# Last stage: the GEGLU's transposes behind the scores, the GEGLU one slot later, and the order of the drain

## The chip, the core and the metric

The kernel runs on one core of one Trainium2 chip, as one launch. The metric is the device time of that launch in microseconds (us). Five engines run beside each other, each in the order of its own instructions: TensorE (PE, whose weight loads the profile lists as PEld), VectorE (DVE), ScalarE (ACT), GpSimd (POOL) and SyncE (SP), which here issues the DMAs. An instruction that needs another engine's result waits on a semaphore, and everything behind it on its own engine waits too.

## The reference

The input x is 8 x 512 x 128, fp32. Two blocks follow each other, each with attention, a residual and a layer norm, then a feed-forward part, a residual and a layer norm. The feed-forward part of the second block, in which the change lies, is itself a small transformer of two layers with windowed attention:

```python
def _layer(x, wqkv, qs, ksc, wo, lg, lb, w1, b1, w2, b2):
    h = shift_token(x)              # half of the features from the token before
    q, k, v = split(h @ wqkv)       # 8 heads of 64
    q, k = l2norm(q) * qs, l2norm(k) * ksc
    q, k = rotary_xpos(q, k)
    x = x + local_attention(q, k, v) @ wo      # windows of 64 tokens and the window before
    h = shift_token(x)
    h = (h - mean) / sqrt(var + 1e-05) * lg + lb
    a, g = split(h @ w1 + b1)       # 341 wide each
    x = x + (a * gelu(g)) @ w2 + b2
    return x
...
x = _layernorm(x + _L1_ffn_ref(x, ...))
```

Its first steps, a layer norm's mean and variance, the product with w1, the gated GELU (GEGLU) and the product with w2, are what the change moves about, together with the last layer norm of all.

## The kernel before, in words

The kernel runs in stages: attention of the first block, its quantized feed-forward part (ffn0), attention of the second block, and the last stage, ffn1, whose function main() holds the change. All activations stay in SBUF: xs and xn, each 128 partitions x 32 chunks of 128 tokens x 128 features. DMAs on the way only move data between partitions.

**Items, chunks and slots.** The last stage has K = 16 items: k = 0 to 7 are the eight batch entries in layer 0, k = 8 to 15 the same in layer 1. An item has NT = 4 chunks of 128 tokens. The loop at L1007 runs over slots t = 1 to 63 with k, c = divmod(t, 4): in one slot each engine gets its instructions for several chunks at different depths of a pipeline. Chunk t begins (the projections to q and k), chunk t-1 is transposed (operands_T), chunk t-2 has its scores and exponentials, chunk t-3 is divided by its sums, chunk t-4 has its weights transposed and multiplied with v, and chunk t-5 gets its output product (sums). All instructions are kept in program order, so the order of the calls in the loop's body is the order on each engine.

**What a slot has, in order.** begin (L1004: PE, q_ps and k_ps), weights_T (L888: PE, p_ps), rotate of q (L713: DVE), over_sums (L865: DVE reciprocal den, POOL product pw), weights_taken (L894: DVE copies pT), scores (L828: PE, sp), squares (L720: ACT), maxima (L847: DVE, m), rotate of k, v_of (L870: PE v_ps, ACT copy v, two DMAs into ve), operands_T (L816: PE, t_ps), operands (L822: ACT copies kT and qT), values (L899: PE, o_ps), sizes (L723: DVE reduction and sum, POOL sum), weights (L854: ACT, eight exponentials pw), norms (L730: POOL floor, power -0.5 and the product with k), values_taken (L912: ACT copy oT), and sums (L916: PE y_ps, DVE additions into xs). The profile names the buffers that q, k and their norms live in was_q, was_k and was_v.

operands_T of chunk t-1 reads what norms of the slot before wrote: its transposes t_ps wait for POOL's last product of that slot.

**Feed-forward part of an item.** It runs two items behind, spread over the slots of item k:
- c = 0, at the end: the shifted input hn of item k-2 is gathered by DMAs (shifted, L692).
- c = 1: normed (L956): statistics of hn on DVE, reciprocal roots (rstd, mr) on POOL, and on POOL the additions of b2, and in layer 1 also of xn, to xs. At the slot's end four ACT instructions normalize hn (L1041).
- c = 2: turned (L963), four PE transposes nT of hn, ahead of the scores; turned_taken, the ACT copy of nT; and geglu (L972) behind the scores: for three chunks of w1 the PE groups gp and ap (two matmuls of 512 columns), a gelu on ACT and a DVE product into u.
- From c = 3 on, sums(t-5, t-11) multiplies u with w2, a chunk per slot.

In layer 1, the slot c = 2 also ends with the moments of the final norm for an item that is complete (DVE and POOL, L1052), and c = 3 with that norm on ACT and its store (finished, L986). PSUM banks for everything but q, k and the scores come from one pool of four (bank, L778).

**The drain**, L1083 to L1118, is the same work written out by hand once no chunk begins any more. E = 14 and L = 15 are the last two items. ended(k) takes the final moments of a batch entry and, with finished, normalizes it on ACT and stores it in one DMA of 256 KB. It is called for E-1 behind normed(L) and scaled(L), for E in the middle of the gates of L, and for L at the very end.

```python
                for n in range(2):
                    for c in range(3):
                        gated(L, c, n)
                    if n == 0:
                        ended(E)
                    for z in range(2):
                        sums(LAST, LAST - 4 + 2 * n + z)
                ended(L)
```

Of the kernel before, what the change touches and what calls it, by code (L numbers as in the profile page):

```python
# [9 lines left out]
F32 = mybir.dt.float32  # L10
# [4 lines left out]
ALU = mybir.AluOpType  # L15
# [3 lines left out]
P = 128  # L19
B, S, D = 8, 512, 128  # L20
NT = S // P
# [30 lines left out]
def body(ctx, tc, x, consts, rows, wa0, wa1, acols, bo, wf, wqkv, wo, w1, w2, cols, b2r, qs, ks, out):  # L52
    nc = tc.nc
# [579 lines left out]
    def ffn1():  # L633
# [139 lines left out]
        def main():  # L773
            with ExitStack() as st:
# [141 lines left out]
                def sums(j, z):  # L916

                    ps, adds = bank("y_ps"), []
                    if 0 <= j < LAST:
                        (k, c), oT = divmod(j, NT), chunk[j].pop("oT")  # L920
                        for i in range(4):
                            mm(ps[:, 0:D], lhsT=oT[:, i, :], rhs=wo_s[:, k // B, i, :], start=(i == 0), stop=(i == 3))
                        adds.append((ps[:, 0:D], (k % B) * NT + c, xs if k >= B else xn))
                    if 0 <= z < LAST:
                        (k, c), u = divmod(z, NT), item[z // NT]["u"]
                        for i, (at, n) in enumerate(H_CH):
                            mm(
                                ps[:, D : 2 * D], lhsT=u[0:n, i, c * P : (c + 1) * P], rhs=w2_s[0:n, k // B, i, :],
                                start=(i == 0), stop=(i == 2),
                            )  # L930
                        adds.append((ps[:, D : 2 * D], (k % B) * NT + c, xs))
                    for y, i, to in adds:
                        v_tt(xs[:, i, :], y, to[:, i, :], ALU.add)


                def moments(x, name):

                    st_ = work.tile([P, NT, 2], F32, tag=f"st{name}", name="st", bufs=1)
                    bn = work.tile([P, NT, 6], F32, tag=f"bn{name}", name="bn", bufs=1)
                    for c in range(NT):  # L940
                        v_stats(bn[:, c, :], x[:, c, :])
                    for c in range(NT):
                        v_aggr(st_[:, c, :], bn[:, c, :])
                    r, m = (work.tile([P, NT], F32, tag=f"{n}{name}", name=n) for n in ("rstd", "mr"))
                    p_ts(r, st_[:, :, 1], LN_EPS, None, ALU.add)
                    p_tt(r, r, half, ALU.pow)
                    p_ts(st_[:, :, 1], st_[:, :, 0], -1.0, None, ALU.mult)
                    p_tt(m, st_[:, :, 1], r, ALU.mult)
                    return r, m

                def normalized(x, dst, shape):
                    r, m = shape
                    for c in range(NT):
                        act(dst[:, c, :], x[:, c, :], AF.Identity, bias=m[:, c : c + 1], scale=r[:, c : c + 1])

                def normed(k):  # L956
# [6 lines left out]
                def turned(k):  # L963
                    item[k]["nT_ps"], hn = bank("nT"), item[k].pop("hn")
                    for c in range(NT):
                        tr(item[k]["nT_ps"][:, c * P : (c + 1) * P], hn[:, c, :], ident)

                def turned_taken(k):
                    item[k]["nT"] = work.tile([P, S], F32, tag="nT", name="nT", bufs=1)
                    copy(item[k]["nT"], item[k].pop("nT_ps"))  # L970

                def geglu(k):  # L972
                    item[k]["u"] = work.tile([P, 3, S], F32, tag="u", name="u", bufs=2)
                    for c in range(3):
                        gated(k, c)

                def gated(k, c, half=None):
                    l, nT, u, (at, n) = k // B, item[k]["nT"], item[k]["u"], H_CH[c]
                    to = slice(0, S) if half is None else slice(half * S // 2, (half + 1) * S // 2)
                    gp, ap = bank("gp")[0:n, to], bank("ap")[0:n, to]  # L980
                    for ps, o in ((gp, HID), (ap, 0)):
                        mm(ps, lhsT=w1_s[:, l, o + at : o + at + n], rhs=nT[:, to], start=True, stop=True)
                    act(u[0:n, c, to], gp, AF.Gelu, bias=cols_s[0:n, l, 3 + c : 4 + c])
                    v_stt(u[0:n, c, to], ap, cols_s[0:n, l, c : c + 1], u[0:n, c, to], ALU.add, ALU.mult)

                def finished(b):  # L986
                    x = slice(b * NT, (b + 1) * NT)
                    normalized(xs[:, x, :], xn[:, x, :], item[B + b].pop("shape"))
                    nc.sync.dma_start(out=ov[:, b], in_=xn[:, x, :])
# [17 lines left out]
                for t in range(1, LAST):  # L1007
                    k, c = divmod(t, NT)
                    if c == 1 and k + 1 < K:
                        load(k + 1)  # L1010
                    begun(t, begin)
                    at_(t - 4, weights_T)
                    if c == 2 and 0 <= k - 2 < K:
                        turned(k - 2)
                    begun(t, squares, 1)
                    if c == 2 and 0 <= k - 2 < K:
                        turned_taken(k - 2)
                    begun(t, rotate, 0)
                    at_(t - 3, over_sums)
                    at_(t - 4, weights_taken)  # L1020
                    at_(t - 2, scores)
                    begun(t, squares, 0)
                    at_(t - 2, maxima)
                    if c == 3 and k + 1 < K:
                        load_T(k + 1)
                    if c == 2 and 0 <= k - 2 < K:
                        geglu(k - 2)
                    if c == 1 and 0 <= k - 2 < K:
                        normed(k - 2)
                    begun(t, rotate, 1)  # L1030
                    at_(t - 2, v_of)
                    at_(t - 1, operands_T)
                    at_(t - 1, operands)
                    at_(t - 4, values)
                    begun(t, sizes)
                    at_(t - 2, weights)
                    begun(t, norms)
                    at_(t - 4, values_taken)
                    if c == 1 and 0 <= k - 2 < K:
                        h = item[k - 2]["hn"]  # L1040
                        normalized(h, h, item[k - 2].pop("shape"))  # L1041
                    sums(t - 5, t - 11)
                    if c == 0 and 0 <= k - 2 < K:
                        hn = work.tile([P, NT, D], F32, tag="hn", name="hn", bufs=1)
                        item[k - 2]["hn"] = shifted(xs[:, rows_of(k - 2), :], hn)
                    if t in (4, 5):
                        scaled_weights(t - 4)
                    if t == 6:
                        tables(1)
                    z = t - 11  # L1050
                    if z >= B * NT and z % NT == NT - 1:
                        item[z // NT]["shape"] = moments(xs[:, rows_of(z // NT), :], "f")  # L1052
                    if z > B * NT and z % NT == 0:
                        finished(z // NT - 1 - B)
# [16 lines left out]
                def begin_hn(k):  # L1071
                    hn = work.tile([P, NT, D], F32, tag="hn", name="hn", bufs=1)
                    item[k]["hn"] = shifted(xs[:, rows_of(k), :], hn)
# [2 lines left out]
                    h = item[k]["hn"]  # L1076
                    normalized(h, h, item[k].pop("shape"))

                def ended(k):
                    item[k]["shape"] = moments(xs[:, rows_of(k), :], "f")  # L1080
                    finished(k - B)

                E, L = K - 2, K - 1  # L1083
                rest(LAST)
# [5 lines left out]
                sums(LAST - 4, LAST - 10)  # L1090
                rest(LAST + 2)
                sums(LAST - 3, LAST - 9)
                turned(E)
                turned_taken(E)
                rest(LAST + 3)
                sums(LAST - 2, LAST)
                sums(LAST - 1, LAST)
                begin_hn(L)
                item[E]["u"] = work.tile([P, 3, S], F32, tag="u", name="u", bufs=2)
                gated(E, 0)  # L1100
                gated(E, 1)
                normed(L)
                gated(E, 2)
                scaled(L)
                ended(E - 1)
                for z in range(4):
                    sums(LAST, LAST - 8 + z)
                turned(L)
                turned_taken(L)
                item[L]["u"] = work.tile([P, 3, S], F32, tag="u", name="u", bufs=2)  # L1110
                for n in range(2):
                    for c in range(3):
                        gated(L, c, n)
                    if n == 0:
                        ended(E)
                    for z in range(2):
                        sums(LAST, LAST - 4 + 2 * n + z)
                ended(L)  # L1118

        return early, main  # L1120

# [177 lines left out]
```

## Time and profile before

| | |
|---|---|
| time, median of 3 runs | 1792.84 us (1790.72 to 1793.9) |
| the profiled execution | 1800.05 us, of which the span of the profile is 1798.2 us |
| mean granted TensorE clock | 0.961 of full speed |
| busy: PE, DVE, ACT, POOL | 92%, 78%, 70%, 50% of the span |
| last stage, 1151 to 1720 us | PE busy 557.1 of 569.0 us, DVE 491.9, ACT 459.2, POOL 473.6, clock 1.00 |
| drain, 1720 to 1798.2 us | PE busy 50.5 of 78.2 us, clock 0.88 |
| one item, layer 0 (1294.40 to 1336.66 us) | 42.26 us: PE busy 41.5, DVE 36.1, ACT 33.7, POOL 34.4 |
| one item, layer 1 (1634.04 to 1677.12 us) | 43.08 us: PE busy 41.9, DVE 38.8, ACT 35.7, POOL 37.3 |

All durations of single instructions come from the profiled execution, which was a little longer than the runs without a profile. A row of the timeline gives the start in us from the span's start, the length in us, the engine, the line (mostly that of a helper, so that the buffers' names tell what it is), the operation, output<-inputs with shapes, and how many were merged; in brackets stands the idle time of the engine ahead of it, and what ended that. PE rows of neighbouring groups overlap a little, since matmuls are pipelined and their ends are modelled. The chain of work that ended last follows the program back from its end, at each step to what released it.

### The profile page before, as it was taken

What the parts mean: (1) busy time and instruction counts of PE and PEld (TensorE: products, weight loads), DVE (VectorE), ACT (ScalarE), POOL (GpSimd) and SP (SyncE); (2) the same over time, 40 slices, a digit from 0 to 9 for tenths busy, and PEclk for the clock granted to TensorE, in tenths of its full rate; (3) what the DMA queues carried; (4) which work ended last, traced back from release to release, by engine and by line L of the source; (5) the groups of instructions that cost most, each with busy time, mean ns of one, the idle gap of its engine ahead of it and who ended that gap; (6) DMA issues with size and microseconds to landing.
All of it is one profiled execution on the core that took longest, in us unless ns stands there. A gap on an engine that the chain in (4) does not pass through costs nothing.

```text
span 1798.2 us, 42058 instructions
## 1 busy us (share of the span) xinstructions
PE 1647.6 (92%) x16305; PEld 955.2 (53%) x16305; DVE 1400.7 (78%) x2220; ACT 1255.9 (70%) x2996; POOL 904.5 (50%) x970
## 2 busy tenths in 40 slices
PE   1699999999997779999999989999999999999984
PEld 0345544555445544444444446566666666666663
DVE  2578778778848788888888857788888888999962
ACT  0177777776764457777878867778878877888862
POOL 3223213332125652323322257887888888888862
PEclk6599999999999989999999999999999999999997
DMA  6833122231110133332322101111111111111110
GB/s 110 210 69 76 37 61 61 60 62 36 14 14 1 41 74 83 67 72 61 62 58 61 40 4 34 34 35 40 38 34 38 35 39 36 40 40 39 34 34 24
DMA packets 92649, 90.27 MB, mean 50 GB/s; under 512 B 45937, under 2 KB 57969, under 8 KB 92450
## 3 DMA queue, kind: packets, MB, share of 16 engines
q1 hardware_dynamic: 87760, 86.57, 21.8%
q8 instruction: 130, 2.13, 0.5%
q0 software_dynamic: 4096, 0.54, 0.2%
q14 instruction: 69, 0.57, 0.1%
q10 hardware_dynamic: 594, 0.47, 0.1%
HBM read 41.85 MB, written 18.87 MB: 34 GB/s over the span
## 4 chain that ended last, share of the span: by engine, by line
PE 70%; DVE 9%; ACT 8%; POOL 6%; DMA 3%; issue 3%; SPq 1%; ACTq 0%; DVEq 0%; POOLq 0%
PE av L250 15%; PE s_ps L250 12%; PE t_ps L250 9%; PE sp L637 5%; PE y_ps L637 4%; PE o_ps L637 2%; PE gp L637 2%; ACT e L48 2%; PE ap L637 2%; PE t_ps L637 2%; DVE m L637 2%; PE o_ps L251 2%; PE p_ps L637 2%; PE q_ps L637 2%; POOL y L465 2%
## 5 line engine op out<-in xcount | busy, mean ns | idle before, releaser
L48 DVE TENSOR_REDUCE m<-s_ps 128x2 f32<-128x1024 f32 x512 | 621.3, 1224 | 174.6 <-PE s_ps L250 170.1
L48 ACT ACTIVATE e<-t_ps 128x512 f32<-128x512 f32 x1024 | 556.1, 596 | 182.1 <-PE t_ps L250 174.1
L250 PE MATMUL av<-e,va 128*32 128x256 f32 x4096 | 328.0, 393 | 10.8 <-ACT avs L48 10.7
L250 PE MATMUL s_ps<-k,q 63*128 63x512 f32 x1024 | 263.6, 510 | 31.3 <-DMA k<-far 24.7
L48 POOL DMA_DIRECT2D q<-mt x128 | 68.8, 541 | 364.1 <-ACT mt L48 364.1
L250 PE MATMUL t_ps<-q,k 64*128 64x512 f32 x1024 | 247.5, 447 | 1.3 <-ACT e L48 1.3
L637 ACT ACTIVATE pw<-sp,m,was_v 128x128 f32<-128x128 f32 x512 | 227.0, 474 | 2.8 <-DVE m L637 1.4
L250 PEld LDWEIGHTS s_ps<-k,q 63*128 63x128 f32 x1024 | 98.9, 188 | 237.9 <-issue 161.5
L637 POOL TENSOR_TENSOR was_v<-was_v 128x16 f32<-128x16 f32 x64 | 187.6, 2931 | 5.3
L250 PEld LDWEIGHTS av<-e,va 128*32 128x32 f32 x4096 | 81.6, 108 | 100.6 <-issue 59.0
L250 PEld LDWEIGHTS t_ps<-q,k 64*128 64x128 f32 x1024 | 122.2, 189 | 22.8 <-ACT e L48 11.1
L637 POOL TENSOR_TENSOR pw<-pw,den 128x1024 f32<-128x1024 f32 x64 | 121.2, 1894 | 8.9 <-DVE den L637 8.9
L637 ACT ACTIVATION_READ_ACCUMULATOR pw<-sp,m,was_v 128x1 f32 x512 | 113.2, 221 | 0.0
L250 PEld LDWEIGHTS <-sel 64*128 64x128 bf16 x2048 | 66.9, 97 | 76.8 <-issue 47.9
L637 DVE TENSOR_REDUCE m<-sp 128x4 f32<-128x512 f32 x128 | 82.2, 683 | 21.8 <-PE sp L637 20.0
L637 ACT COPY v<-v_ps 128x512 f32<-128x512 f32 x64 | 37.5, 586 | 83.4 <-PE v_ps L637 83.4
L637 POOL TENSOR_TENSOR was_k<-was_k,was_q 128x512 f32<-128x512 f32 x64 | 85.5, 1335 | 6.1 <-DVE was_q L637 6.1
L48 POOL CAST parts<-x 128x512 fp32r<-128x512 f32 x32 | 19.4, 607 | 135.5 <-ACT x L48 135.5
L637 PEld LDWEIGHTS t_ps<-cst,was_k 128*128 128x128 f32 x512 | 59.7, 142 | 42.8 <-POOL was_k L637 22.0
L637 DVE COPY pT<-p_ps 128x512 f32<-128x512 f32 x128 | 79.6, 662 | 1.6 <-PE p_ps L637 1.6
L637 PEld LDWEIGHTS p_ps<-cst,pw 128*128 128x128 f32 x512 | 59.8, 141 | 33.1 <-issue 26.1
L637 DVE TENSOR_REDUCE was_v<-was_k 128x16 f32<-128x1024 f32 x64 | 77.0, 1204 | 0.0
(193 smaller groups left out, 3314.1 us busy)
## 6 DMA issues: line engine op xcount, KB each, us to landing
far<-parts SPq DMA_DIRECT2D x64, 256.0 KB
q<-far SPq DMA_DIRECT2D x256, 64.0 KB
k<-far SPq DMA_DIRECT2D x256, 64.0 KB
ve<-v SPq DMA_DIRECT2D x112, 128.0 KB
xn<-in_x SPq DMA_DIRECT2D x8, 256.0 KB
q<-mt POOLq DMA_DIRECT2D x128, 4.0 KB, 2.9
hn<-xs SPq DMA_DIRECT2D x16, 128.0 KB
out<-xn SPq DMA_DIRECT2D x8, 256.0 KB
```

The lines of the kernel that those rows point to most:

```text
L48: return lambda *a, **k: self.tc.keep_in_program_order(f(*a, **k))
L250: mm = lambda *a, **k: tc.keep_in_program_order(nc.tensor.matmul(*a, **k))
L251: tr = lambda *a, **k: tc.keep_in_program_order(nc.tensor.transpose(*a, **k))
L465: kept = lambda f: lambda *a, **k: tc.keep_in_program_order(f(*a, **k))
L637: kept = lambda f: lambda *a, **k: tc.keep_in_program_order(f(*a, **k))
```

## The change

In the loop, turned and turned_taken of item k-2 go behind the scores, the squares, the maxima and (in c = 3) load_T; geglu goes from slot c = 2 to slot c = 3, behind load_T. In the drain, the final moments are split from the norm that uses them (measured and finished in place of ended): measured(E-1) is ahead of turned(E), finished for its batch entry behind begin_hn(L); measured(E) is ahead of the gates of L, finished between their halves. The last batch entry is normalized and stored in two halves of two chunks each, the first half's moments ahead of the last two calls of sums.

```diff
-                def moments(x, name):
+                def moments(x, name, n=NT):
...
-                    for c in range(NT):
+                    for c in range(n):
                         v_stats(bn[:, c, :], x[:, c, :])
-                    for c in range(NT):
+                    for c in range(n):
                         v_aggr(st_[:, c, :], bn[:, c, :])
...
+                    r, m, st_, halves_ = r[:, 0:n], m[:, 0:n], st_[:, 0:n], half[:, 0:n]
...
-                    for c in range(NT):
+                    for c in range(x.shape[1]):
                         act(dst[:, c, :], x[:, c, :], AF.Identity, bias=m[:, c : c + 1], scale=r[:, c : c + 1])
...
                     at_(t - 4, weights_T)
-                    if c == 2 and 0 <= k - 2 < K:
-                        turned(k - 2)
                     begun(t, squares, 1)
-                    if c == 2 and 0 <= k - 2 < K:
-                        turned_taken(k - 2)
                     begun(t, rotate, 0)
...
                     if c == 3 and k + 1 < K:
                         load_T(k + 1)
                     if c == 2 and 0 <= k - 2 < K:
+                        turned(k - 2)
+                        turned_taken(k - 2)
+                    if c == 3 and 0 <= k - 2 < K:
                         geglu(k - 2)
...
-                def ended(k):
+                def measured(k):
                     item[k]["shape"] = moments(xs[:, rows_of(k), :], "f")
-                    finished(k - B)
+
+                def measured_half(n):
+                    at = (B - 1) * NT + 2 * n
+                    return moments(xs[:, at : at + 2, :], "f", 2)
+
+                def finished_half(n, shape):
+                    at = (B - 1) * NT + 2 * n
+                    normalized(xs[:, at : at + 2, :], xn[:, at : at + 2, :], shape)
+                    nc.sync.dma_start(out=ov[:, B - 1, 2 * n : 2 * n + 2], in_=xn[:, at : at + 2, :])
...
                 sums(LAST - 3, LAST - 9)
+                measured(E - 1)
                 turned(E)
                 turned_taken(E)
...
                 begin_hn(L)
+                finished(E - 1 - B)
...
                 scaled(L)
-                ended(E - 1)
...
                 turned_taken(L)
+                measured(E)
                 item[L]["u"] = work.tile([P, 3, S], F32, tag="u", name="u", bufs=2)
-                for n in range(2):
-                    for c in range(3):
-                        gated(L, c, n)
-                    if n == 0:
-                        ended(E)
-                    for z in range(2):
-                        sums(LAST, LAST - 4 + 2 * n + z)
-                ended(L)
+                for c in range(3):
+                    gated(L, c, 0)
+                finished(E - B)
+                for z in range(2):
+                    sums(LAST, LAST - 4 + z)
+                for c in range(3):
+                    gated(L, c, 1)
+                first = measured_half(0)
+                for z in range(2):
+                    sums(LAST, LAST - 2 + z)
+                finished_half(0, first)
+                finished_half(1, measured_half(1))
```

More of the change, by code (lines that the diff above doesn't have):

```diff
@@ L933, in sums @@
                         v_tt(xs[:, i, :], y, to[:, i, :], ALU.add)
-                def moments(x, name):
+                def moments(x, name, n=NT):
                     st_ = work.tile([P, NT, 2], F32, tag=f"st{name}", name="st", bufs=1)
                     bn = work.tile([P, NT, 6], F32, tag=f"bn{name}", name="bn", bufs=1)
-                    for c in range(NT):
+                    for c in range(n):
                         v_stats(bn[:, c, :], x[:, c, :])
-                    for c in range(NT):
+                    for c in range(n):
                         v_aggr(st_[:, c, :], bn[:, c, :])
-                    r, m = (work.tile([P, NT], F32, tag=f"{n}{name}", name=n) for n in ("rstd", "mr"))
+                    r, m = (work.tile([P, NT], F32, tag=f"{f}{name}", name=f) for f in ("rstd", "mr"))
+                    r, m, st_, halves_ = r[:, 0:n], m[:, 0:n], st_[:, 0:n], half[:, 0:n]
                     p_ts(r, st_[:, :, 1], LN_EPS, None, ALU.add)
-                    p_tt(r, r, half, ALU.pow)
+                    p_tt(r, r, halves_, ALU.pow)
                     p_ts(st_[:, :, 1], st_[:, :, 0], -1.0, None, ALU.mult)
```

## The prediction

> **What bounds the kernel now.** I read the page's busy row (PE 92%) and its slices first, the granted clock in tenths among them, then the critical chain between 1080 and 1798 us, then PE's timeline through one work item, then POOL's beside it, last the drain.
>
> ```profile
> PEclk6599999999999989999999999999999999999997
> ```
>
> In the last stage (1151 to 1720 us) PE works 557.1 of 569.0 us at full clock, and the chain is one PE row after another, with a short detour once per item. An item (four slots, c = 0 to 3) takes 42.26 us, and 43.0 us for k = 12 to 15. This is the slot c=2 of one item:
>
> ```profile
> 1362.51 1.04 PE L637 MATMUL p_ps<-cst,pw 128*128 128x128 f32 x8
> 1364.25 0.69 PE L637 MATMUL nT<-cst,hn 128*128 128x128 f32 x4 [0.70 <-ACT hn L637]
> ...
> 1371.59 1.02 PE L637 MATMUL v_ps<-wqkv_s,hT 128*128 128x512 f32 x2
> 1372.45 1.04 PE L637 MATMUL t_ps<-cst,was_k 128*128 128x128 f32 x8
> ```
>
> The detour is the wait of nT for hn: the chain ends p_ps at 1363.39 and starts nT at 1364.25, so 0.86 us. That is what the moved transposes can win. Now POOL over the same time. The product at 1368.31 is the last step of norms for the chunk of slot c=1, and t_ps in slot c=2 transposes its result:
>
> ```profile
> 1360.03 0.23 POOL L637 TENSOR_SCALAR rstd<-st 128x4 f32<-128x4 f32 x1 [1.18 <-DVE st L637]
> ...
> 1361.93 1.27 POOL L637 TENSOR_TENSOR xs<-xs,was_v 128x512 f32<-128x512 f32 x1
> 1363.16 1.73 POOL L637 TENSOR_TENSOR was_k<-was_k,was_q 128x512 f32<-128x512 f32 x1
> 1364.97 0.25 POOL L637 TENSOR_SCALAR was_v<-was_v 128x16 f32<-128x16 f32 x1
> 1365.30 2.93 POOL L637 TENSOR_TENSOR was_v<-was_v 128x16 f32<-128x16 f32 x1
> 1368.31 1.04 POOL L637 TENSOR_TENSOR was_k<-was_k,was_v 128x512 f32<-128x512 f32 x1
> ```
>
> In slot c=1 POOL has the moments of hn and the xs additions ahead of that chunk's norms, so the product ends late, at 1369.35. PE does not feel it, because the six GEGLU groups (5.2 us) lie between scores and t_ps. Elsewhere there is no such room: in slot c=1 the product of c=0 ends at 1356.84 and t_ps starts at 1357.08. The GEGLU is POOL's cover.
>
> **Steady part, items k = 2 to 15.** Moving turned behind scores: PE no longer waits, since the scores take 1.47 us and hn is ready at 1364.56 (1362.88 + 1.68). Gain 0.86 us an item. turned_taken moves with it on ACT: one copy of 0.58, still ahead of the table load, hidden as before. No DMA moves here.
>
> Moving geglu to c=3: the same groups run, one slot later, 5.2 us of PE. But now, in c=2, PE comes to t_ps at 1363.39 + 1.47 (sp) + 0.6 (nT) + 0.86 (v_ps) = 1366.3, and the product lands at 1369.35 plus 0.04 of signal. A new wait of 3.0 us (3.1 unrounded). Behind t_ps on PE are o_ps, y_ps, the next q_ps and k_ps; ACT's kT and qT copies and then its exponentials wait for t_ps, all by the same 3.0. In c=3 I see nothing late: POOL's next product comes 8.2 us behind this one (pw 1.9, ve 0.5, sum 1.3, floor 0.6, power 2.9, product 1.0), PE's next t_ps 14.4 behind the last (t 0.87, o 1.08, y 1.76, q, k and p 2.6, sp 1.4, hT 0.6, groups 5.2, v 0.9); ACT fits its hT copy (0.59), table load (1.28) and gelus under the six groups; sums needs u at the slot's end, 4 us after the last gelu's input. In the slot after geglu, norms ends 8.0 us behind the last group (1379.77 against 1371.75), and PE reaches t_ps there after 9.7 (v 0.86, t 0.87, o 1.08, y 1.76, q, k and p 2.6, sp 1.69, v 0.86).
> - k = 2 to 9: +3.0 - 0.86 = +2.15, times 8 = +17.
> - k = 10, 11: POOL also adds xn (1.60); its product ends at 1497.34, PE would come at about 1493.1: a wait of 4.25, net +3.4, times 2 = +7.
> - k = 12 to 15: also the final norm's moments. The product ends at 1625.67 (the row below), PE would come at 1621.3: 4.4 less the 1.0 that nT waits there, +3.4. These moments now run beside the GEGLU in c=3, so the 0.33 us that c=0 and c=1 each lose now to late products goes (the weight load of t_ps idles 0.94 on POOL was_k at 1602.94 and 1611.98, and these slots take 9.05 instead of 8.72): +2.7, times 4 = +11. If DVE's m row shortens with it (1.73 against 1.28), 2 us less.
>
> ```profile
> 1624.63 1.04 POOL L637 TENSOR_TENSOR was_k<-was_k,was_v 128x512 f32<-128x512 f32 x1
> ```
>
> Sum +35, taken as **+34**, with 28 and 38 as ends.
>
> **The clock.** Such long idle stretches of PE are new to this stage, and the drain shows what they cost. Columns: the window and its length, busy us of each engine, granted clock, DMA.
>
> ```profile
> 1741.65:1745.06 3.41, 2.08 (x19) 1.84 (x19) 2.49 (x13) 3.07 (x14) 1.84 (x5) 1.00 0.17 38
> 1765.47:1768.88 3.41, 0.00 (x0) 0.00 (x0) 0.00 (x0) 1.86 (x5) 1.36 (x3) 1.00 0.00 0
> 1768.88:1772.29 3.41, 3.10 (x7) 2.52 (x8) 0.48 (x1) 0.86 (x3) 0.00 (x0) 0.50 0.27 77
> 1775.71:1779.12 3.41, 1.38 (x7) 0.87 (x5) 0.00 (x0) 1.86 (x5) 1.36 (x3) 1.00 0.00 0
> 1779.12:1782.53 3.41, 3.21 (x10) 2.55 (x11) 1.35 (x3) 0.97 (x3) 0.00 (x0) 0.50 0.29 82
> ```
>
> The granted clock changes in steps of 3.41 us; after a step in which PE was busy 0 or 1.38 us the next is granted half, after 2.08 us it is not. Between, the trace is mixed (1.41 kept it, at 543.5 us), so about 2.0 us idle in one step is my limit. A wait of 3.0 has that in (3.0 + 3.41 - 4.0)/3.41 = 0.7 of the phases, one of 4.3 in all. A half step costs up to 1.7 us; I take 1.4, since some falls into the wait. That is 8 x 0.7 x 1.4 + 6 x 1.4 = 16. New items near 44.4 us are almost 13 steps, so the phase may stick, either way. I take **+14**, with ends 0 and 22.
>
> The Trainium skill ("TensorE: Matmul & The Clock Gate", "Part 1: The HAM clock gate") gives the same step but says that half rate follows at least one idle window. The row with 1.38 us busy differs, and the row decides; by the page's rule a wait of 3.0 would cost nothing and one of 4.3 would cost in a quarter of the phases, an estimate that would make the sum lower by about 12.
>
> **The drain.** Three rows:
>
> ```profile
> 1767.02 1.65 ACT L637 ACTIVATE xn<-xs,mr,rstd 128x128 f32<-128x128 f32 x4 [2.97 <-POOL mr L637]
> ...
> 1769.19 1.22 PE L637 MATMUL gp<-nT,w_s 128*128 128x256 f32 x2 [4.75 <-ACT nT L637]
> ...
> 1786.89 1.65 ACT L637 ACTIVATE xn<-xs,mr,rstd 128x128 f32<-128x128 f32 x4 [5.92 <-POOL mr L637]
> ```
>
> Now ACT holds the nT copy of item L behind a final norm that waits for POOL, and PE idles 4.75 us and loses its clock; the second norm delays the last gelus in the same way (2.23 us), and the third is the end.
> - measured(E-1) earlier: its DVE rows (1.14 us) fall into 1.17 us that DVE idles before pT at 1750.15, its 1.9 us of POOL into 10.96 idle ahead of 1760.44. Cost 0, at most 1. Its norm (1.65 on ACT) delays the first gelu from 1755.52 to 1756.3; the second waits for PE until 1757.23 anyway. Its store moves on SP ahead of nothing but the other stores, and behind hn's four issues (last at 1756.68); beside hn's landing it costs 0 to 1.
> - nT's copy then starts at 1764.45, right behind the transposes, instead of 1768.57: 4.2 gained. PE keeps full clock: six groups of 0.43 (2.6 us) instead of 4.4.
> - measured(E) ahead of the gates runs on DVE and POOL until 1767.1; finished's ACT work (1.65) then lies under sums and the next gates. First u at 1768.2, sums to 1769.1, six groups to 1771.7, last u 1772.3, last addition 1773.7, against 1783.70. Gain 10.0.
> - The end by halves: the second half needs 2 stats and 2 aggregates (0.7) and waits for the first half's POOL chain (to 1775.05), then 1.95 POOL, 0.85 ACT: issue at 1778.0, 4.3 behind the last addition instead of 4.9. The last store is 128 KB instead of 256, whose data moved for about 1.9 us (1789 to 1791): 0.9 less. The tail behind it stays. Slicing moments and normalized to two chunks changes no duration of the other calls.
>
> Together 10.0 + 0.6 + 0.9 = 11.5, taken as **-11**, with ends -6 (a half step strikes, stores collide) and -13.
>
> **Sum.** +34 + 14 - 11 = +37 on the profiled execution (1800.05 us, span 1798.2): 1837. The runs' median is 1792.84, a factor of 0.996: **1830 us**. Ends: 28 + 0 - 13 = +15 and 38 + 22 - 6 = +54, so 1808 to 1847.
>
> **Rivals.**
> - The waits come, the clock holds (0.22): +34 - 11 = +23, 1816. For it: a phase that sticks well. Against: the row with 1.38.
> - The waits are about 1.7 us instead of 3 to 4.4, too short for the clock (0.08): 14 x (1.7 - 0.86) - 11 - 2 = about 0, 1788 to 1806. It needs POOL's chain to shorten by over 1 us, say through less contention with DVE (was_k at 1363.16 takes 1.73 instead of 1.27).
> - **Faster** (0.10): POOL's product is out before PE comes to t_ps in c=2, so only gains stay: 14 x 0.86 + 2.6 + 11 = 26, 1767. The place is that product, the point 1.83 us of wait per item (0.86 plus 13.6/14, the other gains); below it the change wins. For it: POOL idles 1.18 us ahead of rstd in c=1. Against: from rstd on POOL runs without a gap for 9.3 us, and PE needs 6.3 from that start.
>
> The forecast holds 0.60. Signs, with 0.2% either way as what a measurement can tell from no change: the second rival splits 0.04 slower, 0.03 same, 0.01 faster. So faster 0.11, same 0.03, slower 0.86. The range 1803 to 1848 holds the forecast's and the first rival's ends and a little of the second.
>
> **What would show it.** Right: weight loads of t_ps in slot c=2 idle some 3 and 4.3 us on POOL was_k, items of 44 to 47 us, half-clock steps after 1151 us, nT without a wait, the final chain from nT to the last addition 9 to 10 us instead of 19. Wrong: t_ps in c=2 unidle, or idle shifted to c=3, where gelu or u could be late in a way I do not see.

## The result and the profile after

The changed kernel takes **1835.12 us** (median of 4 runs, 1833.65 to 1835.17) against 1793.12 for the kernel before on the same chip (4 runs, 1790.72 to 1793.9): a ratio of 1.0235, 95% interval 1.0219 to 1.0251. It is slower by 42 us; forecast were 1830 us and a range of 1803 to 1848. The profiled execution took 1835.1 us, span 1833.3. First the page: busy row and granted clock.

```profile
PE 1654.3 (90%) x16304; PEld 964.6 (53%) x16305; DVE 1398.5 (76%) x2220; ACT 1256.7 (69%) x2996; POOL 902.5 (49%) x974
...
PEclk6699999999999989999999999999999999999998
```

PE falls from 92% to 90% of a longer span. In tenths the clock row shows next to nothing of what the clock cost; that takes windows as short as its steps. Next PE's timeline through slot c=2 of an item of layer 0, the one whose rows the prediction shows:

```profile
1369.32 0.66 PE L637 MATMUL nT<-cst,hn 128*128 128x128 f32 x4
1369.81 1.02 PE L637 MATMUL v_ps<-wqkv_s,hT 128*128 128x512 f32 x2
1373.85 1.09 PE L637 MATMUL t_ps<-cst,was_k 128*128 128x128 f32 x8 [3.01 <-POOL was_k L637]
```

nT no longer waits. With the GEGLU groups gone from between v_ps and t_ps, PE waits 3.01 us for POOL, whose timeline shows the same order and durations as before; only PE comes earlier:

```profile
1366.37 1.27 POOL L637 TENSOR_TENSOR xs<-xs,was_v 128x512 f32<-128x512 f32 x1
...
1369.74 2.93 POOL L637 TENSOR_TENSOR was_v<-was_v 128x16 f32<-128x16 f32 x1
1372.75 1.04 POOL L637 TENSOR_TENSOR was_k<-was_k,was_v 128x512 f32<-128x512 f32 x1
```

The product ends at 1373.79 and t_ps starts 0.06 us later. In layer 1 the wait is longer and what follows is slow (PE timeline, item k = 12):

```profile
1601.02 1.02 PE L637 MATMUL v_ps<-wqkv_s,hT 128*128 128x512 f32 x2
1606.30 1.97 PE L637 MATMUL t_ps<-cst,was_k 128*128 128x128 f32 x8 [4.25 <-POOL was_k L637]
```

t_ps takes 1.97 us instead of 1.09. The same stretch in windows as long as the clock's steps and 0.1 us behind them (columns: window, length, busy us of PE, PEld, DVE, ACT, POOL, granted clock, DMA share, GB/s):

```profile
1601.00:1604.40 3.40, 1.04 (x4) 0.21 (x2) 3.37 (x8) 1.58 (x3) 3.23 (x3) 0.98 0.16 36
1604.40:1607.80 3.40, 1.50 (x7) 1.51 (x8) 2.39 (x3) 0.35 (x1) 3.32 (x3) 0.50 0.18 42
1607.80:1611.20 3.40, 3.40 (x40) 2.95 (x39) 0.00 (x0) 3.13 (x13) 3.32 (x5) 0.51 0.00 0
1611.20:1614.60 3.40, 3.40 (x21) 2.39 (x21) 2.16 (x12) 2.14 (x8) 3.31 (x2) 1.00 0.02 5
```

The window with PE busy 1.04 us is followed by one at half clock; PE is busy only 1.50 us in that one too, and a second half window follows, in which PE works throughout. The wait of 4.25 us costs two half windows in every item from k = 10 on. In layer 0 the phase, that is where the wait falls among the clock's steps, is kinder: here the wait of 3.01 is split over two steps, with PE busy 2.06 and 1.75 us (1368.77 to 1375.60), and the clock stays. In one item of layer 0 it does not:

```profile
1460.93:1464.34 3.41, 1.53 (x24) 1.36 (x26) 3.38 (x6) 0.84 (x2) 3.33 (x3) 1.00 0.33 77
1464.34:1467.75 3.41, 3.41 (x34) 3.29 (x30) 0.82 (x1) 3.41 (x16) 3.33 (x5) 0.50 0.00 0
```

There the half window is full of work, and a single one follows.

The drain's rows in the changed kernel, from PE's timeline and from ACT's:

```profile
1809.73 0.70 PE L637 MATMUL gp<-nT,w_s 128*128 128x256 f32 x2 [0.68 <-ACT nT L637]
```

```profile
1820.00 0.88 ACT L637 ACTIVATE xn<-xs,mr,rstd 128x128 f32<-128x128 f32 x2 [2.94 <-POOL mr L637]
1822.04 0.88 ACT L637 ACTIVATE xn<-xs,mr,rstd 128x128 f32<-128x128 f32 x2 [1.16 <-POOL mr L637]
```

PE idles 0.68 us ahead of gp instead of 4.75, and the last norm comes in two halves.

**Where the time went**, in us, from the starts of nT (the loop's items k = 2 to 15; E and L are the two in the drain):

| stretch | before | after | difference |
|---|---|---|---|
| start of the span to nT in k = 2 | 1152.20 | 1147.24 | -4.96 |
| layer 0, nT of k = 2 to nT of k = 10 | 338.81 | 357.09 | +18.28 |
| layer 1, nT of k = 10 to nT(E) | 257.28 | 288.31 | +31.03 |
| nT(E) to nT(L) | 15.08 | 15.34 | +0.26 |
| nT(L) to the end of the last addition | 20.33 | 11.13 | -9.20 |
| from there to the end of the span | 14.50 | 14.19 | -0.31 |
| sum | 1798.20 | 1833.30 | +35.10 |

The first line lies ahead of the change; in the twelve traces of this case it runs from 1146.44 to 1152.70. In these two traces the loop lost 49.3 us and the drain gave back 9.25.

### The profile page after: what moved, and what is told of

It reads as the page before. It is cut to its first block, busy times and chain, and to the rows that moved or that the text cites. A ratio compares the mean times of both kernels' runs of the same rounds, so it can differ in the third digit from the quotient of the medians.

```text
span 1833.3 us, 42075 instructions
## 1 busy us (share of the span) xinstructions
PE 1654.3 (90%) x16304; PEld 964.6 (53%) x16305; DVE 1398.5 (76%) x2220; ACT 1256.7 (69%) x2996; POOL 902.5 (49%) x974
## 3 DMA queue, kind: packets, MB, share of 16 engines
HBM read 41.85 MB, written 18.87 MB: 33 GB/s over the span
## 4 chain that ended last, share of the span: by engine, by line
PE 69%; POOL 11%; DVE 7%; ACT 6%; issue 3%; DMA 3%; SPq 1%; ACTq 0%; DVEq 0%; POOLq 0%
PE av L250 15%; PE s_ps L250 11%; PE t_ps L250 9%; PE y_ps L637 4%; PE sp L637 4%; POOL was_v L637 3%; PE o_ps L637 3%; PE t_ps L637 3%; ACT e L48 2%; POOL was_k L637 2%; PE gp L637 2%; PE ap L637 2%; PE o_ps L251 2%; PE p_ps L637 2%; PE q_ps L637 2%
## 5 line engine op out<-in xcount | busy, mean ns | idle before, releaser
L637 PE MATMUL t_ps<-cst,was_k 128*128 128x128 f32 x512 | 72.5, 288 | 53.6 <-POOL was_k L637 52.7
L637 POOL TENSOR_SCALAR was_v<-was_v 128x16 f32<-128x16 f32 x64 | 28.6, 447 | 126.8 <-DVE was_v L637 125.6
```

The costliest lines, as they stand in the source:

```text
L637: kept = lambda f: lambda *a, **k: tc.keep_in_program_order(f(*a, **k))
```

## The experiments

Medians in us; the ratio is to the kernel before on the same chip, with its 95% interval; the last two columns are nT to nT of an item, without k = 2 and k = 15. Where no wait of t_ps for POOL is left in slot c=2, k = 10 still takes as long as layer 0 and is left out of the last column.

| kernel | median | before | ratio | item, layer 0 | item, layer 1 |
|---|---|---|---|---|---|
| the change | 1835.12 | 1793.12 | 1.0235 [1.0219, 1.0251] | 44.48, once 46.05 | 47.83 to 48.20 |
| loop_only | 1853.1 | 1797.68 | 1.0313 [1.0277, 1.0350] | 44.48 to 47.24 | 47.83 to 48.19 |
| drain_only | 1785.32 | 1797.68 | 0.9943 [0.9927, 0.9959] | 42.27 | 43.02 to 43.19 |
| adds_late | 1793.45 | 1797.68 | 0.9990 [0.9973, 1.0006] | 43.14 | 43.13 |
| warm | 1828.99 | 1797.68 | 1.0189 [1.0157, 1.0220] | 44.50 to 46.06 | 45.74 |
| geglu_alone | 1831.79 | 1796.39 | 1.0195 [1.0167, 1.0223] | 44.51 | 45.77 to 47.30 |
| turned_alone | 1791.21 | 1796.39 | 0.9966 [0.9951, 0.9982] | 42.50 | 43.16 to 43.38 |
| v_first | 1773.63 | 1796.39 | 0.9864 [0.9838, 0.9889] | 41.28 | 41.84 to 42.36 |
| v_first_adds_late | 1775.43 | 1796.39 | 0.9878 [0.9856, 0.9899] | 41.28 | 41.84 to 42.27 |
| store_behind | 1769.97 | 1797.01 | 0.9862 [0.9842, 0.9883] | 41.28 | 41.85 to 42.36 |
| whole_end | 1770.06 | 1797.01 | 0.9863 [0.9833, 0.9893] | 41.28 | 41.85 to 42.51 |

My theory was the prediction's: t_ps comes to POOL's product too early, and the clock adds to that. The rivals: the moved transposes are what costs; the new drain is.

### loop_only and drain_only: which half of the change

loop_only is the kernel before with the loop's part of the diff, drain_only the changed kernel with that part undone.

> The changed loop with the drain of before. Theory P (t_ps in slot c=2 waits for POOL's product of norms, and in layer 1 the half clock comes on top): the loop costs all of the 42 us and what the new drain gives back, which the two traces put at about 9 us (from nT of the last item to the end 25.3 us instead of 34.8): 1844 us, with waits of 3.0 us (k = 2 to 9) and 4.25 us (k = 10 to 15) as in the changed kernel. Rival Q (a part of the loss lies in the new order of the drain): below 1838.

> The loop of before with the new drain. P: the drain is a gain by itself, 1793 - 9 = 1784 us, with items of 42.26 and 43.0 us as before and the idle time of PE ahead of the last gates falling from 4.75 to under 1 us. Q: 1790 or more.

The loop's part alone costs 3.13%, the drain's alone gains 0.57%. loop_only is slower than the change by more than the drain explains: half-clock steps struck five items of layer 0 there (45.9 to 47.2 us each), one in the change. Its waits are the same (3.01 to 3.03 and 4.24). Items of 44.48 us are 13.03 steps of 3.413, so the phase hardly moves from item to item. That the stages ahead decide where it stands is my reading, not tried.

### adds_late: is it POOL's product

The additions of b2 and xn go behind norms in slot c=1, so the product no longer waits for them.

```diff
                 def normed(k):
                     item[k]["shape"] = moments(item[k]["hn"], "h")
+
+                def biased(k):
...
                     begun(t, norms)
+                    if c == 1 and 0 <= k - 2 < K:
+                        biased(k - 2)
```

> The changed kernel, but POOL's additions of b2 and xn to xs in slot c=1 come behind norms instead of ahead of them; same work. P: the product of norms ends earlier by the additions (1.27 us, and 1.27 + 1.6 in layer 1), so the waits of t_ps in c=2 fall from 3.0 to about 1.75 us and from 4.25 to about 1.4 us, too short for a half-clock step; items of about 43.2 and 42.9 us instead of 44.5 and 47.8: 1835 - 8 x 1.27 - 6 x 4.9 = 1795 us (1789 to 1803). Rival S (the loss is in slot c=3, where GEGLU's gelus, table loads and products now meet the transposes hT and sums): unchanged, 1828 to 1840.

PE's timeline, then POOL's:

```profile
1361.57 1.02 PE L637 MATMUL v_ps<-wqkv_s,hT 128*128 128x512 f32 x2
1364.26 1.09 PE L637 MATMUL t_ps<-cst,was_k 128*128 128x128 f32 x8 [1.67 <-DVE m L637]
```

```profile
1363.16 1.04 POOL L637 TENSOR_TENSOR was_k<-was_k,was_v 128x512 f32<-128x512 f32 x1
1364.16 1.28 POOL L637 TENSOR_TENSOR xs<-xs,was_v 128x512 f32<-128x512 f32 x1
```

The wait falls from 3.01 (layer 0) and 4.25 (layer 1) to 1.67 us in both, no half-clock step strikes the steady part (nT of k = 2 to nT of k = 15), and the time is that of the kernel before: most of the loss was POOL's additions standing ahead of that product, once PE has nothing to do in the meantime. The drain's gain is in that time, so the loop still loses some 0.5%: 43.14 us an item against 42.27 in drain_only. The profile puts the remaining 1.67 down to DVE's m, which ended at 1364.23. But POOL's product ends at 1364.20, 0.06 ahead of t_ps as in the change, and the weight load that starts t_ps names it:

```profile
1364.26 0.86 PEld L637 LDWEIGHTS t_ps<-cst,was_k 128*128 128x128 f32 x8 [2.49 <-POOL was_k L637]
```

So the product most likely ends this wait too.

### warm: the clock's share in layer 1

The change, with three extra identical products for v ahead of t_ps in slot c=2 from k = 10 on: added work, the same result. PE is busy while it waits.

```diff
-                    at_(t - 2, v_of)
+                    at_(t - 2, v_of, 3 if c == 2 and k >= 10 else 0)
```

> The changed kernel, but for k = 10 to 15 PE does v's product in slot c=2 four times instead of once (the same values into the same bank; three more of 0.86 us each, ahead of the waiting t_ps). The result is the same; it is extra work. P with the clock as its own cause: the extra 2.6 us lie inside the wait of 4.25, which shrinks to 1.7, the window is no longer idle enough, t_ps, o_ps and y_ps behind it run at full clock and items take 45.5 instead of 47.8 us: 1835 - 6 x 2.3 = 1821 us. Rival R (the wait is all, the granted clock costs nothing): 1835, items of 47.8 us. Rival S: slower by 6 x 2.6 = 16 us, 1850, since PE has no room.

```profile
1604.92 3.60 PE L637 MATMUL v_ps<-wqkv_s,hT 128*128 128x512 f32 x8
1610.22 1.09 PE L637 MATMUL t_ps<-cst,was_k 128*128 128x128 f32 x8 [1.69 <-POOL was_k L637]
```

2.6 us more of PE work per item made each item of layer 1 **shorter**, 45.74 instead of 47.83 to 48.20. t_ps still starts when POOL allows it (5.79 us behind nT here, 5.77 in the change), now at full clock. So the clock cost 2.1 us an item and the wait itself 2.7 (45.74 against 43.05). The whole fell by less than the 14 us expected: layer 0, whose code is that of the change, lost its clock in four items here (45.95 to 46.67 us each) against one.

### geglu_alone and turned_alone: which of the two moves

geglu_alone puts the transposes back to their old place; turned_alone leaves the GEGLU in slot c=2, right behind the moved transposes. Both have the new drain.

```diff
 # geglu_alone, against the change
                     at_(t - 4, weights_T)
+                    if c == 2 and 0 <= k - 2 < K:
+                        turned(k - 2)
...
 # turned_alone, against the change
                         turned_taken(k - 2)
-                    if c == 3 and 0 <= k - 2 < K:
                         geglu(k - 2)
```

> The changed kernel with the transposes nT back ahead of the scores; GEGLU stays in slot c=3. Theory P: t_ps in c=2 starts when POOL's product is out, at the same time as in the changed kernel; the transposes' own wait for hn (0.7 to 0.85 us) comes back and the wait of t_ps shrinks by as much, to about 2.2 us (k = 2 to 9) and 3.3 us (k = 10 to 15). Items of 44.5 and 45.5 to 47.8 us, total as the changed kernel, 1835 us (1822 to 1845; the split idle time may lose fewer half-clock steps). Rival T (it is the place of the transposes that costs): near the drain alone, 1785.

> The changed kernel with GEGLU back in slot c=2, right behind the transposes, which stay behind the scores. P: no wait of t_ps for POOL (the 5.2 us of GEGLU cover it), no wait of nT for hn, but the first gp now waits for ACT's copy of nT (0.58 us and its signals, some 0.65 us of PE), so that of the 0.86 us only 0.2 are won: items of 42.05 and 42.8 us, total as the drain alone less 3: about 1782 us. Rival T: the waits of 3 and 4 us stay, 1835.

```profile
1374.18 0.70 PE L637 MATMUL nT<-cst,hn 128*128 128x128 f32 x4 [0.80 <-ACT hn L637]
1379.34 1.09 PE L637 MATMUL t_ps<-cst,was_k 128*128 128x128 f32 x8 [1.94 <-POOL was_k L637]
```

In geglu_alone nT waits 0.80 for hn and t_ps 1.94 for POOL, and the item takes 44.51 us, as with the transposes moved (44.48). Once the product is the bound, the moved transposes win nothing: PE only waits at another place. The loss is the GEGLU's move alone. In layer 1 t_ps waits 3.15 to 3.21 here. Five of the six items lose one half step each, with PE busy all through it, and take 47.1 to 47.3 us; the sixth keeps the clock and takes 45.77. So one half step costs about 1.5, and where the half window is full of work no second one follows.

turned_alone I had wrong: I expected 42.05 us an item and it took 42.50, 0.24 more than before. PE's timeline and ACT's:

```profile
1359.42 0.66 PE L637 MATMUL nT<-cst,hn 128*128 128x128 f32 x4
1361.06 1.12 PE L637 MATMUL gp<-nT,w_s 128*128 128x512 f32 x2 [0.98 <-ACT nT L637]
```

```profile
1359.93 0.60 ACT L637 ACTIVATE was_k<-q_ps 128x512 f32<-128x512 f32 x1 [0.40 <-DVE was_q L637]
1360.42 0.58 ACT L637 COPY nT<-nT 128x512 f32<-128x512 f32 x1
```

The scores used to hide ACT's copy of nT. Without them gp waits 0.98 us for it, and the copy itself stands behind squares of q, which waited 0.40 for DVE's rotation.

### v_first: both covers kept

The gap asks for PE work that needs neither nT nor POOL. v_of of the same slot, 0.86 us, is such work; it goes between the transposes and the groups.

```diff
                         turned_taken(k - 2)
+                        at_(t - 2, v_of)
                         geglu(k - 2)
...
-                    at_(t - 2, v_of)
+                    if c != 2 or k < 2:
+                        at_(t - 2, v_of)
```

> As turned_alone, but v's product goes between the transposes and GEGLU in slot c=2, so that its 0.86 us of PE cover the copy of nT. P: PE waits neither for hn nor for the copy, and t_ps comes 8.1 us behind p_ps, after POOL's product (6.0 us in layer 0, 7.3 in layer 1): items of 41.4 us (k = 2 to 9) and 42.1 us (k = 12 to 15, where the two waits of 0.33 us in c=0 and c=1 stay): the drain alone less 14 x 0.86 = 12 us: about 1773 us, faster than before by over 1%. Rival: ACT's v copy ahead of the gelus delays these and PE's banks, 1785.

> v_first and, as in adds_late, POOL's additions behind norms. P: in v_first the product of norms in c=1 has room already, so the additions' place costs nothing there; behind norms they only push POOL's next product pw by 1.3 to 2.9 us, which PE needs a slot later: as v_first within 3 us, 1773. Rival: POOL is what bounds layer 1 as a whole, and a shorter chain in c=1 takes off another 0.3 us or more per item there: 1770 or less.

```profile
1355.01 0.66 PE L637 MATMUL nT<-cst,hn 128*128 128x128 f32 x4
1355.50 1.02 PE L637 MATMUL v_ps<-wqkv_s,hT 128*128 128x512 f32 x2
1356.36 1.10 PE L637 MATMUL gp<-nT,w_s 128*128 128x512 f32 x2
...
1361.59 1.04 PE L637 MATMUL t_ps<-cst,was_k 128*128 128x128 f32 x8
```

In layer 0 no wait is left in the slot. The item takes 41.28 us, 0.98 less than before, and the kernel beats both others by a clear margin: 0.9864 [0.9838, 0.9889]. Moving POOL's additions on top of that (v_first_adds_late) changes nothing: with the groups as cover the product is not awaited.

### store_behind and whole_end: two terms of the drain

From v_first. store_behind keeps the four gathers of hn(L) and the store of batch entry E-1 in the order of the code; whole_end undoes the halves.

```diff
 # store_behind
-                    item[k]["hn"] = shifted(xs[:, rows_of(k), :], hn)
+                    item[k]["hn"] = shifted(xs[:, rows_of(k), :], hn, kept(nc.sync.dma_start))
...
-                finished(E - 1 - B)
+                finished(E - 1 - B, kept(nc.sync.dma_start))
 # whole_end
-                first = measured_half(0)
...
-                finished_half(0, first)
-                finished_half(1, measured_half(1))
+                measured(L)
+                finished(L - B)
```

> The base is v_first (median ratio 0.9864). Only the drain's DMA order is changed: the four issues that gather hn of item L and the store of batch entry E-1 are kept in the order of the code, so the store comes behind the gather on SP. In the changed kernel and in v_first SP issues the store behind the first of the four (1737.09, 0.38 us long, the next gather 0.48 us later than without it), against the prediction's statement that it comes behind all four. Theory A, the store's place costs: from the last addition that hn needs (1736.77 in v_first) to the first statistics of hn (1741.76) it is 4.99 us, against 4.51 in the kernel before (1754.66 to 1759.17); here 4.5, and from nT of item E to nT of item L 14.9 instead of 15.41. Rival B, the store's data or DVE's earlier moments are what costs: the 4.99 stays within 0.1. The whole time changes by 0.5 us at most, which the runs cannot tell: ratio 0.986, and the trace decides.

> The base is v_first. Only the halves at the very end are undone: the last batch entry gets its moments, norm and store as one of four chunks behind the last addition, as in the kernel before. The prediction gave the halves 1.5 us (0.6 between the last addition and the store's issue, 0.9 in the store). From the start of the last addition to the end of the span it is 14.5 us in the kernel before (1783.70 to 1798.2) and 14.5 in v_first (1756.77 to 1771.3) and in the changed kernel (1818.82 to 1833.3). Theory A, the halves give nothing, since what they save is lost at the program's end: 14.5 here too, ratio as v_first, 0.986 to 0.987. Rival B, they give the 1.5 us and something else in the new drain took it away: 16.0 here, ratio 0.0008 higher. Where the issue itself stands is read apart from that: about 4.9 us behind the last addition's start instead of 4.4.

**store_behind** missed both expectations: statistics of hn start 5.34 us behind the start of the last addition (1737.45 to 1742.79), later than 4.99, and nT(E) to nT(L) takes 15.69 us instead of 14.9. SP's issues, in the changed kernel and here (start, length, the queue's instructions):

```profile
1798.24 0.76 SPq L697 DMA_DIRECT2D hn<-xs  x1
1799.10 0.38 SPq L990 DMA_DIRECT2D out<-xn  x1
1799.58 1.65 SPq L696 DMA_DIRECT2D hn<-xs  x2
...
```

```profile
1737.80 3.15 SPq L637 DMA_DIRECT2D hn<-xs  x4
1741.00 0.63 SPq L637 DMA_DIRECT2D out<-xn  x1
```

L698 follows at 1801.28 for 0.69 us. In the change the gather of L697, which reads only the first three chunks, is issued 0.54 us before the last addition starts (1798.78), and the store behind it. SP does not follow the code's order here, against what the section on the kernel says of all instructions. In the code's order that early start is lost (all four issues wait for the last addition), which costs more than the store's place. The two effects come apart by the last gather's issue: from its end to the statistics it is 1.81 us in the kernel before (1757.36 to 1759.17), 1.84 in the change, 1.81 in v_first and 1.84 here, wherever the store and its data are. So the store costs its 0.48 us on SP's queue (the next gather comes 1.34 us behind the first instead of 0.86), and its data cost nothing that shows.

**whole_end**: from the start of the last addition to the end of the span 14.74 us (14.53 in v_first). Like the kernel before from there (1783.41 to 1798.2, 14.79; the 14.5 in the expectation was counted from that addition's end). The halves gain 0.2 us, not 1.5. Their parts: the last norm ends 4.12 behind the last addition's start instead of 5.13; the store's data have gone 1.46 behind that instead of 1.95 (window view, by 0.1 us); and from there to the end it is 8.95 instead of 7.65. In that last part SP waits for PE's queue at the program's end, 7.4 us at most in every kernel with the halves and 6.6 in every kernel without (SP's waits, here whole_end):

```profile
SPq L1309 <- PEq L1309: 7.1, 2, 6.6
```

Why this wait grows was not tried. Neither kernel's time differs from v_first's.

## Why the prediction came out right

Sign and mechanism held, and the total nearly. Inside the term of the clock two parts were off in opposite directions, and that their sum came out is luck.

- **New wait in layer 0**: 3.0 us given, 3.01 measured; +2.15 an item given, +2.2 measured. The row that carried it, POOL's product, is what adds_late moves.
- **New wait in layer 1**: 4.25 given, 4.25 measured, net +2.7 from k = 12 on, 2.7 by warm (for k = 10 and 11 +3.4 each, by warm 3.5 and 2.7). The weight loads of t_ps in c=0 and c=1 no longer idle 0.94, as the prediction had it. Only c=1 got shorter by that, 8.72 us from t_ps to t_ps instead of 9.05; c=0 takes 9.06 as it now does in layer 0 too (before: 8.99 in layer 1, 8.72 in layer 0). There the slot behind the GEGLU, c=3 before, loses 0.34 us in its scores, and that loss has moved along.
- **The 0.86 us that the transposes gain**: right as arithmetic, wrong as a gain. geglu_alone shows that under the new bound they are worth nothing (44.51 against 44.48): the wait of 3.0 was that much longer because of them. Alone, without the GEGLU's move, they cost 0.24 (turned_alone).
- **All waits**: the loop's 49.3 less the clock's 14.7 (below) leaves 34.6; taken was 34. In the 34.6 is one more half step, behind the loop (1788.61), which warm has too (1768.16).
- **The clock**: summed to 16 and taken as +14, measured 14.7, but the split failed. Layer 0: 7.8 given (0.7 of 8 items), one half step in fact, 1.6 us. The prediction named the reason, a phase that sticks at 13 steps, and could not know which way. Layer 1: 8.4 given (one half step of 1.4 in each of 6 items), 13.1 in fact (the items less 45.74, for the last less 46.48), since two half windows follow each wait. The step that failed is "a half step costs up to 1.7 us; I take 1.4", counted once per wait: it did not ask whether the half window itself holds enough work to lift the clock. With PE busy 1.50 of 3.40 it doesn't; the size of a single half step, about 1.5 in geglu_alone, was right. How much hangs on the phase: the same loop took 364.3 us for layer 0 in loop_only, 357.1 in the change.
- **The limit of 2.0 us idle in a step** was a little high: 1.66 and 1.80 idle kept the clock (1372.18 and 1191.29), but 1.88 lost it (1460.93), the change's one half step in layer 0. The Trainium skill ("TensorE: Matmul & The Clock Gate", "Part 1: The HAM clock gate") asks for an idle window; a window with PE busy 1.04 of 3.40 us was enough here, and the measurement decides.
- **The drain**: -11 taken, -9.25 measured. nT's copy and the last addition: 10.0 given, 9.20 measured. The store of E-1: "behind hn's four issues", 0 to 1; it is behind the first of them and cost 0.48. The table's +0.26 for this stretch compares two different loops. With the same loop on both sides the stretch is 0.91 us longer (drain_only 15.99, before 15.08) and 1.06 (the change 15.34, loop_only 14.28); what lies beside the store's 0.48 falls ahead of the last addition, and its cause stays open. From nT(E) to the end the new drain then gains 8.5 us (49.89 to 41.35 and 49.14 to 40.68), not 9.25. The end by halves: 0.6 + 0.9 given, 0.2 (whole_end against v_first) to 0.3 measured. The gain up to the norm was 1.0 and that of the store 0.5; the term that was missing is the longer end of the program, 1.2 to 1.3.
- **Against the median**: 37 us given on the profiled execution, 42 measured between the medians. 3.1 of the 5 are the loop (49.3 for 48) and the drain (9.25 for 11); the rest lies in the stages ahead, which differ between executions.

The faster rival named the right place, POOL's product, and about the right point: it was to decide from 1.83 us of wait, and adds_late with 1.67 is level with the kernel before (0.9990). v_first, which keeps the cover and takes the gain, is where that side was to be had.

## What to carry to other kernels

Work that stands between a producer's late step and its consumer is a cover, even if it has nothing to do with either; before moving it, read off when the late result lands and what the consumer's engine has left to do until then. A wait that a move takes away is a gain only if the next wait isn't the same one seen from another place, so add up to the next releaser and not to the next instruction. Where a stretch waits for an engine with a gated clock, count the steps at half clock one after the other, including whether the slow step itself holds enough work to end the slow clock.

## What the runs showed of the hardware

- **What loses the clock, and what brings it back.** In the twelve traces, in the steps of 3.41 us between 1150 us and the end of the loop: after a step at full clock with PE busy up to 1.53 us the next one is granted half, from 1.58 us on it is not; one step with 1.44 kept the clock (loop_only, 1149.11). After a half step with PE busy up to 2.60 us the next is half again, from 3.15 us on it is full. So a wait that still takes some 0.8 us of the half step costs a second one.

- **The clock locks the items.** In layer 1 the items shrink from one to the next, 48.20, 48.00, 47.89, 47.84, 47.83 in the change and 48.19, 48.00, 47.89, 47.85, 47.83 in loop_only, towards 47.79, the distance of the half windows' starts (1652.08, 1699.86, 1747.65), which is 14 steps of 3.413. That the wait sets itself against the steps is my reading; the series is what is shown.
- **POOL's power -0.5 costs by the column**, about 0.16 us each on top of some 0.4: 0.72 us for two columns, 1.04 for four, 2.93 for sixteen. It is the longest step ahead of the product that t_ps waits for.

- **One more DMA in the last store** (two of 128 KB instead of one of 256) went with 0.8 us more of waiting at the program's end (6.6 to 7.4). With it the part of the end behind the store's data grew by 1.3 us, which took back most of what the halves had won.
